# Row sums of the adjacency: added up over tiles by VectorE and GpSimd, with TensorE summing over partitions alone

## The chip, the core and the metric

The kernel runs on one core of a Trainium2 chip. A core has five engines that work side by side, each with its own queue of instructions in a fixed order: TensorE (PE in the profile, with its weight loads as PEld), VectorE (DVE), ScalarE (ACT), GpSimd (POOL) and SyncE (SP), which here only starts transfers. They wait for one another through semaphores. Data lies in SBUF and in the matmul banks of PSUM, both of 128 partitions[...]. The metric is the device time of one execution in microseconds (us), from the first to the last instruction.

## What is computed

Four graph layers run one after the other over x, 16 batches (B) of 1024 nodes (N) with 256 features (D), with one adjacency matrix adj of 1024 x 1024 per batch, all in fp32. Each layer normalises x, applies relu, computes an update and adds it to x. The change touches the first two layers, cut here to what matters:

```
h  = relu(layernorm(x))                              # layer 0
hw = h @ W_w.T + W_b
u  = adj * exp(e[:, None] + f[None, :] + a_b)        # f = hw @ a2
x  = x + (u / sum(u, axis=2)) @ hw

h  = relu(layernorm(x))                              # layer 1
d  = (sum(adj, axis=-1) + 1e-5) ** -0.5
x  = x + (d[:, None] * adj * d[None, :]) @ (h @ weight) + bias
```

In layer 0 the factor exp(e) cancels between u and its row sum, so with g = exp(f) the kernel needs, per batch, the weighted row sum sum_m adj[n, m] g[m] (the denominator, "den") and the plain row sum sum_m adj[n, m] (the degree, "deg"). Layer 1 takes its scale from the degree, layer 2 its inverse. Layers 2 (a gated recurrence over nodes) and 3 (two dense matmuls) are untouched.

## The kernel before, in words

`layers_0_1` goes over the batches in a software pipeline. Iteration i does layer 0 of batch i, then layer 1 of batch i-1, and, between the parts of layer 1, `reshape` of batch i (what layer 1 will need) and `prepare` of batch i+1 (what layer 0 will need). `turn` transposes the output of layer 1 of batch i-2 for layer 2. A scheduler that comes with the tile framework fixes the order of the instructions on each engine when the kernel is built; it may move an instruction past others that it doesn't depend on. At run time each engine keeps its order, whatever waits.

A batch's adjacency lies transposed in SBUF as the tile `at`: eight tiles of 128 source nodes m (the partitions) by 1024 target nodes n. `load` fetches x and `at` on SyncE's queue, in that order: one transfer for x, four for pairs of `at` tiles. `at` has three buffers, x four. A buffer is loaded anew when the last reader of its old content is done.

`prepare` (L169) has three steps. The first takes layernorm statistics on VectorE (L133, L134), and the inverse root on GpSimd (`rs`, L68). The second makes the relu q and, with L178, the dot product f on VectorE, and adds a bias to x on GpSimd (L180); ScalarE makes g = exp(f) (L182), which it writes into column 0 of a tile `gs` of 32 columns per adjacency tile. Column 1 of `gs` holds ones, the others zeros. The third multiplies rs by g (`rg`, L185) on VectorE and scales q with that on ScalarE (L187).

`layer_0` (L190) first makes the row sums on TensorE (`pd`, L196): for each half of the target nodes, eight matmuls with 32 stationary columns of `gs`, one per adjacency tile, four of them side by side in TensorE's column groups (32 columns each). The result lies in PSUM as rows: row 32k has a part of den and row 32k+1 a part of deg. ScalarE copies it to `ds` (L198). Then come the neighbour sums in four parts (`sums`, L147 to L158): a part is eight matmuls of 512 columns into one of two PSUM banks `pa`, which ScalarE (L155) or VectorE (L157) copies to `ag`; a part can begin when the bank of the part before the last has been copied. Eight small matmuls with `sel` (L206) then turn `ds` into columns, one target node per partition, and add the four row groups. VectorE takes the reciprocal of den (L208) and a copy of deg (L210), and the projection by w0 (L214) is added to x with that scale (L215). From deg come `dis_v` (L64), `dis` by GpSimd (L68) and, for layer 2, `safe` (L220 to L225).

`layer_1` has four more such parts, its own projection (L251, L252), the stores x_d and he_d by GpSimd (L254, L258) and the statistics in between. So in the order of VectorE, `prepare` of the next batch lies between the parts of layer 1, and so do the copies of the `pa` banks.

A matmul in fp32 shows as two instructions in the profile, so the 16 matmuls of the row sums show as 32.

Of the kernel before, what the change touches and what calls it, by code (L numbers as in the profile page):

```python
# [9 lines left out]
F32 = mybir.dt.float32  # L10
AF = mybir.ActivationFunctionType
ALU = mybir.AluOpType
AX = mybir.AxisListType
# [3 lines left out]
P = 128  # L17
B, N, D, H = 16, 1024, 256, 1024
NT = N // P
# [19 lines left out]
def gnn_stack(ctx: ExitStack, tc: tile.TileContext, a: dict, out: bass.AP):  # L39
    nc = tc.nc  # L40
# [3 lines left out]
    ident = const.tile([P, P], F32, name="ident")  # L44
    make_identity(nc, ident)
    ones = const.tile([P, P], F32, name="ones")
# [10 lines left out]
    def rows(ap):  # L57
        return ap.rearrange("(t p) d -> p t d", p=P)

    def inv_sqrt(pool, src, eps, shape, name, mul=1.0):  # L60

        t = pool.tile(shape, F32, name=name + "_v")
        if mul == 1.0:
            nc.vector.tensor_scalar(t, src, eps, None, op0=ALU.add)  # L64
        else:
            nc.vector.tensor_scalar(t, src, mul, eps, op0=ALU.mult, op1=ALU.add)
        r = pool.tile(shape, F32, name=name)
        nc.gpsimd.tensor_tensor(r, t, mhalf.to_broadcast(shape), ALU.pow)  # L68
        return r
# [23 lines left out]
    def layers_0_1():  # L93
        with ExitStack() as st:
            wp = st.enter_context(tc.tile_pool(name="w01", bufs=1))
            big = st.enter_context(tc.tile_pool(name="big01", bufs=1))
            small = st.enter_context(tc.tile_pool(name="small01", bufs=2))
            psum = st.enter_context(tc.tile_pool(name="psum01", bufs=2, space=PSUM))
# [19 lines left out]
            v = wp.tile([P, D + 1], F32, name="v")  # L118
            nc.vector.tensor_copy(v, pv)

            gs = [wp.tile([P, NT, 32], F32, name=f"gs{i}") for i in range(2)]
            for g in gs:
                nc.vector.memset(g, 0.0)
                nc.vector.memset(g[:, :, 1:2], 1.0)
            sel = wp.tile([P, 2], F32, name="sel")
            nc.vector.tensor_reduce(sel, ident.rearrange("p (q r) -> p r q", r=32)[:, :2], AX.X, ALU.add)

            def stats(x):

                mv = small.tile([P, NT, 2], F32, name="mv")  # L130
                for t in range(NT):
                    s6 = small.tile([P, 6], F32, name="s6", bufs=4)
                    nc.vector.bn_stats(s6, x[:, t])  # L133
                    nc.vector.bn_aggr(mv[:, t], s6)  # L134
                rs = inv_sqrt(small, mv[:, :, 1], LN_EPS, [P, NT], "rs")
                return mv, rs
# [10 lines left out]
            def sums(at, h, ag):  # L147

                def part(n0, c):
                    pa = psum.tile([P, 512], F32, name="pa")  # L150
                    for mt in range(NT):
                        nc.tensor.matmul(pa, h[:, mt, c * P : (c + 1) * P], at[:, mt, n0 : n0 + 512],  # L152
                                         start=mt == 0, stop=mt == NT - 1)
                    if c == 0:
                        nc.scalar.copy(ag[:, c, n0 : n0 + 512], pa)  # L155
                    else:
                        nc.vector.tensor_copy(ag[:, c, n0 : n0 + 512], pa)  # L157
                return [lambda n0=n0, c=c: part(n0, c) for n0 in (0, 512) for c in range(DC)]  # L158

            at, x, q, g, h1, h2, dis = {}, {}, {}, {}, {}, {}, {}  # L160

            def load(b):
                x[b] = big.tile([P, NT, D], F32, name="x", bufs=4)
                nc.sync.dma_start(x[b], rows(a["x"][b]))
                at[b] = big.tile([P, NT, N], F32, name="at", bufs=3)
                for t in range(0, NT, 2):
                    nc.sync.dma_start(at[b][:, t : t + 2], rows(a["adjT"][b])[:, t : t + 2])

            def prepare(b):  # L169

                mv, rs = stats(x[b])
                yield
                q[b] = big.tile([P, NT, D], F32, name="q")
                f = small.tile([P, NT], F32, name="f")
                for t in range(NT):
                    nc.vector.tensor_scalar(q[b][:, t], x[b][:, t], mv[:, t, 0:1], 0.0, op0=ALU.subtract, op1=ALU.max)
                    junk = small.tile([P, D], F32, name="junk")
                    nc.vector.scalar_tensor_tensor(junk, q[b][:, t], rs[:, t : t + 1], v[:, :D],  # L178
                                                   op0=ALU.mult, op1=ALU.mult, accum_out=f[:, t : t + 1])
                    nc.gpsimd.tensor_tensor(x[b][:, t], x[b][:, t], vec["W_b"], ALU.add)  # L180
                g[b] = gs[b % 2]
                nc.scalar.activation(g[b][:, :, 0], f, AF.Exp, bias=v[:, D : D + 1])  # L182
                yield
                rg = small.tile([P, NT], F32, name="rg")
                nc.vector.tensor_mul(rg, rs, g[b][:, :, 0])  # L185
                for t in range(NT):
                    nc.scalar.activation(q[b][:, t], q[b][:, t], AF.Copy, scale=rg[:, t : t + 1])  # L187
                yield

            def layer_0(b, between):  # L190
                ds = big.tile([P, N], F32, name="ds")
                for n0 in (0, 512):
                    pd = psum.tile([P, 512], F32, name="pd")
                    for mt in range(NT):
                        k = mt % 4
                        nc.tensor.matmul(pd[32 * k : 32 * (k + 1)], g[b][:, mt], at[b][:, mt, n0 : n0 + 512],  # L196
                                         start=mt < 4, stop=mt >= 4)
                    nc.scalar.copy(ds[:, n0 : n0 + 512], pd)  # L198
                ag = big.tile([P, DC, N], F32, name="ag", bufs=2)
                for part in sums(at[b], q[b], ag):  # L200
                    part()
                    if between:
                        between.pop(0)()
                pn = psum.tile([P, NT, 2], F32, name="pmm")
                for nt in range(NT):
                    nc.tensor.matmul(pn[:, nt], ds[:, nt * P : (nt + 1) * P], sel, start=True, stop=True)  # L206
                rc = small.tile([P, NT], F32, name="rc")
                nc.vector.reciprocal(rc, pn[:, :, 0])  # L208
                deg = small.tile([P, NT], F32, name="deg")
                nc.vector.tensor_copy(deg, pn[:, :, 1])  # L210
                for nt in range(NT):
                    po = psum.tile([P, D], F32, name="pmm")
                    for c in range(DC):
                        nc.tensor.matmul(po, ag[:, c, nt * P : (nt + 1) * P], w0[:, c], start=c == 0, stop=c == DC - 1)  # L214
                    nc.vector.scalar_tensor_tensor(x[b][:, nt], po, rc[:, nt : nt + 1], x[b][:, nt],  # L215
                                                   op0=ALU.mult, op1=ALU.add)

                dis[b] = inv_sqrt(small, deg, DEG_EPS, [P, NT], "dis")
                zero = small.tile([P, NT], F32, name="zero")
                nc.vector.tensor_scalar(zero, deg, 0.0, None, op0=ALU.is_equal)  # L220
                safe = small.tile([P, NT], F32, name="safe")
                nc.vector.tensor_add(safe, deg, zero)
                nc.vector.reciprocal(safe, safe)
                nc.vector.tensor_scalar(zero, zero, -1.0, 1.0, op0=ALU.mult, op1=ALU.add)
                nc.vector.tensor_mul(safe, safe, zero)  # L225
                return safe
# [49 lines left out]

            nothing = lambda: None
            load(0)
            for _ in prepare(0):
                pass  # L280
# [506 lines left out]
    def layer_3():  # L787
        with ExitStack() as st:
# [113 lines left out]
            for b in range(B):  # L902
# [21 lines left out]
                nc.gpsimd.dma_start(rows(out[b]), x[b])  # L924

    layers_0_1()
    layer_2()
    layer_3()
# [49 lines left out]
```

## Time and profile before

Three runs took 5647.23, 5647.41 and 5648.99 us, the median 5647.41; the profiled run took 5646.3, its span 5644.6.

| what | us |
|---|---|
| PE busy (whole span) | 5215.2 (92%) |
| DVE busy | 2638.4 (47%) |
| POOL busy | 1418.8 (25%) |
| row sums `pd`, L196, 512 instructions | 62.1 |
| turn to columns, L206, 256 instructions | 29.5 |
| neighbour sums of layers 0 and 1, L152, 2048 instructions | 907.4 |
| idle time of PE before L152, for VectorE's copy L157 | 34.9 |
| one iteration in the middle of the stage | 78.94 |

A row of the groups reads: line, engine, operation, output and inputs, shapes, count, then busy time and mean ns, then the idle time of the engine just before these instructions and who ended it. Busy time of TensorE is an upper reading, since matmuls are pipelined; the distance from start to start in the timeline is the better measure of what a group costs. The window tables give the clock that TensorE was granted (1.00 is full).

### The profile page before, as it was taken

To read this page: it belongs to the slowest core of one execution; us is meant where nothing else is said; L and a number is where in the kernel's file an instruction comes from. 1 tells how busy PE (TensorE), PEld (TensorE's weight loads), DVE (VectorE), ACT (ScalarE), POOL (GpSimd) and SP (SyncE) were. 2 spreads that over 40 slices of the span, in tenths; PEclk is the share of its full clock that TensorE was granted. 3 is DMA by queue.
4 is the path that set the end of the run, shared out by engine and by line. 5 is a ranking of instruction groups with operands and counts; after the bars stand their busy time and mean duration, and the time that the engine had idled before them with its cause. 6 is when DMAs were issued, how large, how long until landed. Compare 5 with 4: busy or idle time off the path is not lost. (4 is left out here: it accounts for less than half of the span.)

```text
span 5644.6 us, 63144 instructions
## 1 busy us (share of the span) xinstructions
PE 5215.2 (92%) x22975; PEld 3637.5 (64%) x22975; DVE 2638.4 (47%) x6386; ACT 1393.6 (25%) x2970; POOL 1418.8 (25%) x1823
## 2 busy tenths in 40 slices
PE   6999999995799998999889999998869999999999
PEld 3455554553687787878778788787645655556555
DVE  3454444532254555555545455555544343343433
ACT  1221112110122222222222222222223232222322
POOL 2232222220111212212121211212124243342422
PEclk9999999997899999999999999999989999999999
DMA  3322332215623333233143333321032212122210
GB/s 127 117 106 77 119 119 112 92 51 154 194 81 122 86 96 100 72 109 87 55 119 93 115 92 99 105 79 40 10 126 90 92 65 105 53 105 82 75 52 16
DMA packets 471994, 520.25 MB, mean 92 GB/s; under 512 B 49793, under 2 KB 419457, under 8 KB 469377
## 3 DMA queue, kind: packets, MB, share of 16 engines
q1 hardware_dynamic: 445440, 430.75, 23.6%
q0 software_dynamic: 26112, 84.03, 4.1%
q8 instruction: 227, 3.72, 0.3%
q14 instruction: 215, 1.75, 0.1%
HBM read 430.70 MB, written 83.95 MB: 91 GB/s over the span
## 5 line engine op out<-in xcount | busy, mean ns | idle before, releaser
L414 PE MATMUL pf<-ab,hb 128*128 128x128 f32 x3648 | 517.7, 284 | 46.7 <-DMA hb<-he_d 34.4
L414 PEld LDWEIGHTS pf<-ab,hb 128*128 128x128 f32 x3648 | 492.2, 199 | 80.9 <-issue 41.1
L852 PE MATMUL ph<-ag,w 128*128 128x512 f32 x1024 | 480.4, 612 | 34.6 <-DVE hh L856 34.5
L152 PE MATMUL pa<-at,h 128*128 128x512 f32 x1024 | 459.0, 602 | 34.9 <-DVE ag L157 34.9
L837 PE MATMUL pa<-at,h 128*128 128x512 f32 x1024 | 455.1, 595 | 29.6 <-DMA at<-in_adjT 29.6
L152 PE MATMUL pa<-at,q 128*128 128x512 f32 x1024 | 448.4, 594 | 0.0
L890 PE MATMUL po<-w,hh 128*128 128x256 f32 x2048 | 447.7, 379 | 0.0
L890 PEld LDWEIGHTS po<-w,hh 128*128 128x128 f32 x2048 | 387.8, 190 | 59.3 <-issue 7.9
L152 PEld LDWEIGHTS pa<-at,h 128*128 128x128 f32 x1024 | 194.8, 193 | 272.3 <-issue 224.3
L852 PEld LDWEIGHTS ph<-ag,w 128*128 128x128 f32 x1024 | 179.2, 190 | 295.6 <-DVE hh L856 151.5
L837 PEld LDWEIGHTS pa<-at,h 128*128 128x128 f32 x1024 | 194.0, 191 | 261.9 <-issue 259.9
L629 DVE TENSOR_TENSOR r<-r,x 128x256 f32<-128x256 f32 x450 | 187.3, 428 | 336.6 <-ACT r L628 336.6
L152 PEld LDWEIGHTS pa<-at,q 128*128 128x128 f32 x1024 | 191.1, 190 | 237.3 <-issue 237.3
L858 POOL TENSOR_TENSOR ss<-ss,sq 128x512 f32<-128x512 f32 x224 | 305.1, 1362 | 116.0 <-ACT sq L855 111.5
L586 PE MATMUL pr<-dx,wh 128*128 128x256 f32 x1288 | 312.7, 386 | 7.5 <-DVE dx L603 7.4
L744 POOL TENSOR_TENSOR ho<-ho,dh 128x512 f32<-128x512 f32 x64 | 81.2, 1269 | 940.0 <-DVE dh L647 785.0
L628 ACT ACTIVATE r<-pr 128x256 f32<-128x256 f32 x450 | 148.2, 381 | 644.7 <-PE pr L586 600.9
L586 PE MATMUL pz<-wh,dx 128*128 128x256 f32 x1288 | 304.7, 379 | 0.0
L586 PE MATMUL pc<-wh,drx 128*128 128x256 f32 x1288 | 304.5, 379 | 0.0
L157 DVE COPY ag<-pa 128x512 f32<-128x512 f32 x64 | 44.2, 690 | 488.0 <-PE pa L152 488.0
L586 PEld LDWEIGHTS pc<-wh,drx 128*128 128x128 f32 x1288 | 244.6, 190 | 33.6 <-DVE drx L631 0.3
L586 PEld LDWEIGHTS pr<-dx,wh 128*128 128x128 f32 x1288 | 235.8, 193 | 46.8 <-issue 13.6
(170 smaller groups left out, 8480.6 us busy)
## 6 DMA issues: line engine op xcount, KB each, us to landing
at<-in_adjT SPq DMA_DIRECT2D x128, 1024.0 KB
ab<-in_adj SPq DMA_DIRECT2D x128, 512.0 KB
x<-in_x SPq DMA_DIRECT2D x16, 1024.0 KB
x_d<-x POOLq DMA_DIRECT2D x16, 1024.0 KB, 7.9
he_d<-h POOLq DMA_DIRECT2D x16, 1024.0 KB, 7.9
heT_d<-hT POOLq DMA_DIRECT2D x16, 1024.0 KB, 4.2
he<-heT_d SPq DMA_DIRECT2D x16, 1024.0 KB
hb<-he_d SPq DMA_DIRECT2D x16, 1024.0 KB
```

The costliest lines, as they stand in the source:

```text
L152: nc.tensor.matmul(pa, h[:, mt, c * P : (c + 1) * P], at[:, mt, n0 : n0 + 512], start=mt == 0, stop=mt == NT - 1)
L157: nc.vector.tensor_copy(ag[:, c, n0 : n0 + 512], pa)
L414: nc.tensor.matmul(pb[:, c], hb[:, j, c * P : (c + 1) * P], ab[:, j], start=j == jts[0], stop=j == jts[-1])
L586: nc.tensor.matmul(to, lhsT, rhs, start=False, stop=True, skip_group_check=True)
L628: nc.scalar.activation(r[:, e], pr[:, e], AF.Sigmoid)
L629: nc.vector.tensor_mul(r[:, e], r[:, e], x[:, e])
L744: nc.gpsimd.tensor_tensor(ho, ho, dh, ALU.add)
L837: nc.tensor.matmul(pa, h[b][:, mt, c * P : (c + 1) * P], at[b][:, mt, n0 : n0 + NH], start=mt == 0, stop=mt == NT - 1)
L852: nc.tensor.matmul(ph, w1[:, c, k * P : (k + 1) * P], ag[:, c, n0 : n0 + NH], start=c == 0, stop=c == DC - 1)
L858: nc.gpsimd.tensor_tensor(ss, ss, sq, ALU.add)
L890: nc.tensor.matmul(po, hh[:, c, k * P : (k + 1) * P], w2[:, c], start=c == 0, stop=c == HC - 1)
```

## The change

The sum over m is split. Over the eight tiles it is done away from TensorE: VectorE builds den by scaling the first tile with g and adding the other seven with one multiply-add each, and GpSimd builds deg by seven additions. Both lie in a tile `both` of two rows of 1024 values per partition, in one buffer. TensorE is left with the sum over the 128 partitions: four matmuls with 32 columns of ones, each with its own 512 values and its own column group, after the second part of the neighbour sums instead of ahead of the first. The turn to columns then takes four matmuls with four columns of the identity. To make room in SBUF, x has three buffers instead of four, and the `gs` tiles and the two-buffer `ds` go away. The change is meant to free TensorE of most of the row sums.

```diff
--- before.py
+++ after.py
@@ -118,12 +118,9 @@
             v = wp.tile([P, D + 1], F32, name="v")
             nc.vector.tensor_copy(v, pv)
 
-            gs = [wp.tile([P, NT, 32], F32, name=f"gs{i}") for i in range(2)]
-            for g in gs:
-                nc.vector.memset(g, 0.0)
-                nc.vector.memset(g[:, :, 1:2], 1.0)
-            sel = wp.tile([P, 2], F32, name="sel")
-            nc.vector.tensor_reduce(sel, ident.rearrange("p (q r) -> p r q", r=32)[:, :2], AX.X, ALU.add)
+
+            sel = wp.tile([P, 4], F32, name="sel")
+            nc.vector.tensor_copy(sel, ident[:, ::32])
 
             def stats(x):
 
@@ -157,10 +154,10 @@
                         nc.vector.tensor_copy(ag[:, c, n0 : n0 + 512], pa)
                 return [lambda n0=n0, c=c: part(n0, c) for n0 in (0, 512) for c in range(DC)]
 
-            at, x, q, g, h1, h2, dis = {}, {}, {}, {}, {}, {}, {}
+            at, x, q, both, h1, h2, dis = {}, {}, {}, {}, {}, {}, {}
 
             def load(b):
-                x[b] = big.tile([P, NT, D], F32, name="x", bufs=4)
+                x[b] = big.tile([P, NT, D], F32, name="x", bufs=3)
                 nc.sync.dma_start(x[b], rows(a["x"][b]))
                 at[b] = big.tile([P, NT, N], F32, name="at", bufs=3)
                 for t in range(0, NT, 2):
@@ -178,36 +175,44 @@
                     nc.vector.scalar_tensor_tensor(junk, q[b][:, t], rs[:, t : t + 1], v[:, :D],
                                                    op0=ALU.mult, op1=ALU.mult, accum_out=f[:, t : t + 1])
                     nc.gpsimd.tensor_tensor(x[b][:, t], x[b][:, t], vec["W_b"], ALU.add)
-                g[b] = gs[b % 2]
-                nc.scalar.activation(g[b][:, :, 0], f, AF.Exp, bias=v[:, D : D + 1])
+                g = small.tile([P, NT], F32, name="g")
+                nc.scalar.activation(g, f, AF.Exp, bias=v[:, D : D + 1])
                 yield
                 rg = small.tile([P, NT], F32, name="rg")
-                nc.vector.tensor_mul(rg, rs, g[b][:, :, 0])
+                nc.vector.tensor_mul(rg, rs, g)
                 for t in range(NT):
                     nc.scalar.activation(q[b][:, t], q[b][:, t], AF.Copy, scale=rg[:, t : t + 1])
+                both[b] = big.tile([P, 2, N], F32, name="both")
+                den, deg = both[b][:, 0], both[b][:, 1]
+                nc.gpsimd.tensor_tensor(deg, at[b][:, 0], at[b][:, 1], ALU.add)
+                nc.vector.tensor_scalar(den, at[b][:, 0], g[:, 0:1], None, op0=ALU.mult)
+                for t in range(1, NT):
+                    nc.vector.scalar_tensor_tensor(den, at[b][:, t], g[:, t : t + 1], den, op0=ALU.mult, op1=ALU.add)
+                    if t > 1:
+                        nc.gpsimd.tensor_tensor(deg, deg, at[b][:, t], ALU.add)
                 yield
 
             def layer_0(b, between):
-                ds = big.tile([P, N], F32, name="ds")
-                for n0 in (0, 512):
-                    pd = psum.tile([P, 512], F32, name="pd")
-                    for mt in range(NT):
-                        k = mt % 4
-                        nc.tensor.matmul(pd[32 * k : 32 * (k + 1)], g[b][:, mt], at[b][:, mt, n0 : n0 + 512],
-                                         start=mt < 4, stop=mt >= 4)
-                    nc.scalar.copy(ds[:, n0 : n0 + 512], pd)
                 ag = big.tile([P, DC, N], F32, name="ag", bufs=2)
-                for part in sums(at[b], q[b], ag):
+                for i, part in enumerate(sums(at[b], q[b], ag)):
                     part()
                     if between:
                         between.pop(0)()
-                pn = psum.tile([P, NT, 2], F32, name="pmm")
-                for nt in range(NT):
-                    nc.tensor.matmul(pn[:, nt], ds[:, nt * P : (nt + 1) * P], sel, start=True, stop=True)
+                    if i == 1:
+                        pd = psum.tile([P, 512], F32, name="pd", bufs=1)
+                        for k in range(4):
+                            nc.tensor.matmul(pd[32 * k : 32 * (k + 1)], ones[:, :32],
+                                             both[b][:, k // 2, k % 2 * 512 : (k % 2 + 1) * 512], start=True, stop=True)
+                        ds = small.tile([P, 512], F32, name="ds", bufs=1)
+                        nc.scalar.copy(ds, pd)
+                pn = psum.tile([P, NT // 2, 4], F32, name="pmm")
+                for t in range(NT // 2):
+                    nc.tensor.matmul(pn[:, t], ds[:, t * P : (t + 1) * P], sel, start=True, stop=True)
+
                 rc = small.tile([P, NT], F32, name="rc")
-                nc.vector.reciprocal(rc, pn[:, :, 0])
+                nc.vector.reciprocal(rc.rearrange("p (h t) -> p t h", h=2), pn[:, :, :2])
                 deg = small.tile([P, NT], F32, name="deg")
-                nc.vector.tensor_copy(deg, pn[:, :, 1])
+                nc.vector.tensor_copy(deg.rearrange("p (h t) -> p t h", h=2), pn[:, :, 2:])
                 for nt in range(NT):
                     po = psum.tile([P, D], F32, name="pmm")
                     for c in range(DC):
```

## The prediction

> **What bounds the kernel now.** Layers 0 and 1 fill the first 1318 us; the diff touches nothing later, so I carry the rest over unchanged. I read first the busy table of one steady iteration of this stage (iteration 7, from the end of the layer-1 sums, T0 = 562.60 us, to the next such end, 641.54). Columns: window, length, then PE, PEld, DVE, ACT, POOL busy with counts, PE clock, DMA share, GB/s.
>
> ```profile
> 562.60:641.54 78.94, 76.47 (x259) 40.02 (x258) 37.00 (x110) 15.95 (x33) 21.67 (x24) 1.00 0.29 107
> ```
>
> TensorE is busy 76.47 of 78.94 us. VectorE (37.0), GpSimd (21.7) and DMA (29%) are far from full: work taken from TensorE shortens the iteration, unless what replaces it sits in front of something TensorE waits for. So I read TensorE's timeline (start, length, group):
>
> ```profile
> 569.52 3.64 PE L196 MATMUL pd<-at,gs 128*32 128x512 f32 x32
> 573.09 14.00 PE L152 MATMUL pa<-at,q 128*128 128x512 f32 x32
> ...
> 602.41 1.84 PE L206 MATMUL pmm<-sel,ds 128*128 128x2 f32 x16
> 604.12 1.11 PE L214 MATMUL pmm<-w,ag 128*128 128x256 f32 x4
> ...
> 618.08 13.90 PE L152 MATMUL pa<-at,h 128*128 128x512 f32 x32
> 634.45 7.13 PE L152 MATMUL pa<-at,h 128*128 128x512 f32 x16 [2.47 <-DVE ag L157]
> ```
>
> The row sums are the first line (3.57 us start to start) and their turn to columns is the third (1.71 us). The last line is the iteration's only gap: 2.47 us, for VectorE's copy of a PSUM bank (L157). The timelines of VectorE and GpSimd show why that copy is late, and what they do to each other:
>
> ```profile
> 570.82 0.51 DVE L64 TENSOR_SCALAR rs_v<-mv 128x8 f32<-128x8 f32 x1
> ...
> 629.14 0.47 DVE L178 SCALAR_TENSOR_TENSOR junk<-q,rs,v 128x256 f32<-128x256 f32 x1
> ...
> 630.95 0.93 DVE L178 SCALAR_TENSOR_TENSOR junk<-q,rs,v 128x256 f32<-128x256 f32 x1
> ...
> 633.62 0.17 DVE L185 TENSOR_TENSOR rg<-rs,gs 128x8 f32<-128x8 f32 x1 [0.37 <-ACT gs L182]
> 633.71 0.69 DVE L157 COPY ag<-pa 128x512 f32<-128x512 f32 x1
> ```
>
> ```profile
> 570.41 0.95 POOL L254 DMA_DIRECT2D x_d<-x  x1 [18.09 <-DVE mv L134]
> ...
> 629.97 1.63 POOL L180 TENSOR_TENSOR x<-x,W_b_sb 128x256 f32<-128x256 f32 x2 [1.05 <-DVE q L176]
> ```
>
> The copy stands in VectorE's queue behind all of `prepare`, a chain that began with the reciprocal at 604.29 and runs almost without rest to 633.71: in this half VectorE sets the pace. And VectorE slows beside GpSimd: L178 takes 0.47 us alone, 0.93 beside a GpSimd add; the tiny L64 takes 0.51 us, ending as GpSimd's instruction does (elsewhere L64 is 0.15).
>
> Last, the clock after such a gap (same columns):
>
> ```profile
> 236.38:239.80 3.42, 3.42 (x6) 1.39 (x7) 0.00 (x0) 3.14 (x8) 0.00 (x0) 0.66 0.00 0
> ...
> 634.45:637.85 3.40, 3.40 (x8) 1.63 (x9) 0.00 (x0) 3.15 (x8) 0.00 (x0) 1.00 0.00 0
> ```
>
> After 5 of the 14 gaps (155.97, 236.38, 553.81, 871.57, 1110.08 us) the clock halves for a while and the 16 matmuls take 8.60 to 8.83 us instead of 7.13; after the other 9 it doesn't.
>
> [...]
>
> **The change part by part**, per steady iteration:
>
> *Removed from TensorE.* pd goes from 32 instructions to 8 (4 matmuls of two passes, still four column groups): 8 x 3.57/32 = 0.9, say 1.0 us with its start, so -2.6. The turn goes from 16 to 8 instructions: -0.85. Together -3.4 us.
>
> *Added to VectorE, ahead of the copy.* As built, VectorE's order after L185 is: the first scaling (L188 of the changed file), two multiply-adds (L190), then the bank copy TensorE waits for, then five more L190. Each L190 waits for the one before it (in place), so they don't overlap. [...] 0.74 + 1.27 + 1.2 = +3.2 us on the gap. [...] GpSimd is then idle (its last add ends at 632.96), so 3.2. Behind the copy, the other five (6.4 us) are hidden under the last seven-us part of the sums.
>
> *A longer gap.* 2.47 + 3.2 = 5.7 us[...]; before it was 5 x 1.7/14 = 0.6. +0.85; bounds 0 and 1.7.
>
> *Added to GpSimd.* Seven adds of 1024 columns. From L494 (256 columns 732 ns, 128 columns 460): 2.1 ns a column, so 2.35 us[...]; I take 2.4 with the wait on its own result, 17 us in all. GpSimd's order as built: he_d store of i-2, the seven adds for batch i+1, heT_d store, `dis` of batch i. `both` has one buffer, so the adds wait for pd of batch i: they run an iteration ahead of their use, and TensorE never waits for them. But when do they end? pd ends at T0+23. Their tile comes later than before: with three x buffers, x[i+1] may load only when h2 of batch i-2 is done (T0+15), and adjT queues behind x in the same queue. Data then starts near T0+16.7, x and he_d (2 MB) and the first adjT pair (1 MB) at the 400 GB/s of the busiest slices take 8 us: T0+24.7. So the adds run from T0+24.7 to T0+41.7. TensorE's turn now ends 3.4 us sooner, at T0+38.1, and VectorE reaches `dis_v`, `zero` and `safe` (tiny single-source and two-input SBUF operations, L64 and after) at T0+39.6. They'd sit behind the last add, as L64 did behind the store: +2.1 us. Queued behind them: the second x update (L215), for which the third PSUM bank of the projection waits, and the whole chain to the copy. So the delay goes through to the end of the iteration. Bounds: 0 (adds end by T0+39.6) and 4.
>
> *At no cost:* `sel`, the memsets (once), the strided reciprocal (8 elements), one pd bank instead of two (read once per iteration), the ds copy (ACT is idle), x with three buffers (x lands by T0+23, first read near T0+47).
>
> Sum: -3.4 + 3.2 + 0.85 + 2.1 = +2.75 us, for iterations 2 to 14: +35.8. Iterations 0 and 1: -6.8 for TensorE, +1.4 because the sums start after the first scaled q where pd started with g, +3[...], +3 of delay at `dis`, +3.2 of gap: +3.8. Iteration 15 has no `prepare` and no adds: -3.4. Total +36: 5683 us.
>
> **The rivals.** (1) [...]the adds end in time, or the tiny operations slip between them. 13 x 0.65 + 0.8 - 3.4 = +6: 5653. For it: during `dis` on GpSimd (605.91 to 607.58) the tiny L222 ran in 0.15. Against: `dis` is 8 elements; the adds stream 1024. (2) *Faster*: the gap grows by 2.5 only and the clock stays, 13 x -0.9 - 3 - 3.4 = -18: 5629. For it: the 9 gaps with full clock. Against: VectorE's order is fixed, and the gap more than doubles. (3) *Adds much later*: adjT lands 2 us later, or the adds are slowed by VectorE, delay 4 to 5: 13 x 5.2 + 3.8 = +71: 5718. For it: L178 once took 2.89 us beside three short GpSimd operations. Against: little of VectorE runs then.
>
> **How the numbers follow.** Forecast 0.52, rival 1 0.23, rival 2 0.12, rival 3 0.13. Point 5683. The range leaves out the outer halves of rivals 2 and 3: 5636 to 5714. Within 0.2% is 5636 to 5659: most of rival 1, the edge of rival 2, 0.18. Faster 0.14, slower 0.68.
>
> **What would show it.** TensorE: pd 8 instructions in about 1 us, the turn 0.9. The gap before the last L149 part, released by VectorE's copy, near 5.7 us, with clock near 0.5 for some of the next 3.4 us. L64 of `dis_v` or L225 stretched to 1 to 2.5 us, ending as an add ends, and TensorE waiting 2 us inside the projection. Wrong if the gap stays near 2.5, if the adds end before the turn, or if TensorE waits at pd for GpSimd.

## The result and the profile after

The changed kernel took 5668.93 us (median of six runs, 5649.84 to 5681.16), the kernel before 5647.32 beside it: a ratio of 1.0039, 95% interval 1.0021 to 1.0057. It is slower by some 22 us, so the forecast had the direction and its range holds the time; 5683 was 14 us too high. How much of the working was right is another matter, and the profile tells it.

First the window table of one iteration after the change (columns as in the prediction: window, length, busy times with counts of PE, PEld, DVE, ACT, POOL, clock, DMA share, GB/s), with the first 3.4 us after one of the gaps:

```profile
568.03:571.43 3.40, 3.40 (x4) 1.50 (x5) 3.33 (x3) 0.00 (x0) 0.00 (x0) 0.50 0.00 0
...
496.40:577.40 81.00, 75.30 (x227) 39.36 (x226) 46.57 (x118) 15.35 (x32) 38.05 (x31) 0.96 0.29 104
```

The iteration is 81.0 us long, where one took 78.9 before (79.6 in the mean, with the clock losses), with 32 fewer TensorE instructions. VectorE has 9.6 us more work and GpSimd 16.4, yet neither is anywhere near full. TensorE's timeline of the same iteration (T0, the end of the layer-1 sums, is 496.4) shows where the time went:

```profile
487.91 8.55 PE L149 MATMUL pa<-at,h 128*128 128x512 f32 x16 [5.71 <-DVE ag L154]
496.30 7.11 PE L256 MATMUL pmm<-w,ag 128*128 128x256 f32 x32
...
517.95 1.07 PE L204 MATMUL pd<-both,ones 128*32 128x512 f32 x8
...
533.66 0.95 PE L210 MATMUL pmm<-sel,ds 128*128 128x4 f32 x8
534.47 1.11 PE L219 MATMUL pmm<-w,ag 128*128 128x256 f32 x4
...
568.03 9.44 PE L149 MATMUL pa<-at,h 128*128 128x512 f32 x16 [5.70 <-DVE ag L154]
```

From T0 to the end of the turn it is 38.1 us where it was 41.5: TensorE's saving is there in full, 3.5 us. From the end of the turn to the start of the gap it is 27.9 us in both kernels: no delay arises there. The gap is 5.70 us instead of 2.46, and the 16 matmuls behind it take 9.44 us instead of 7.13. All 14 gaps cost clock now; the durations behind them run 8.55, 9.44, 9.90, 10.13, and again 8.55. VectorE's timeline holds the cause of the gap and, for this iteration, the absence of the predicted delay:

```profile
535.62 0.48 DVE L220 SCALAR_TENSOR_TENSOR x<-pmm,rc,x 128x256 f32<-128x256 f32 x1 [0.72 <-PE pmm L219]
536.02 0.16 DVE L64 TENSOR_SCALAR dis_v<-deg 128x8 f32<-128x8 f32 x1
...
536.50 0.15 DVE L227 TENSOR_TENSOR safe<-deg,zero 128x8 f32<-128x8 f32 x1
...
563.90 0.17 DVE L182 TENSOR_TENSOR rg<-rs,g 128x8 f32<-128x8 f32 x1 [0.37 <-ACT g L179]
563.99 0.75 DVE L188 TENSOR_SCALAR both<-at,g 128x1024 f32<-128x1024 f32 x1
564.77 2.60 DVE L190 SCALAR_TENSOR_TENSOR both<-at,g,both 128x1024 f32<-128x1024 f32 x2
567.29 0.68 DVE L154 COPY ag<-pa 128x512 f32<-128x512 f32 x1
```

The three operations between `rg` and the copy make up the added 3.2 us. `dis_v` and `safe` are not stretched here. GpSimd's timeline says why, and the issues on SyncE's queue say where its timing comes from:

```profile
519.14 2.33 POOL L187 TENSOR_TENSOR both<-at 128x1024 f32<-128x1024 f32 x1 [6.60 <-PE pd L204]
521.55 14.47 POOL L192 TENSOR_TENSOR both<-both,at 128x1024 f32<-128x1024 f32 x6
535.96 0.59 POOL L279 DMA_DIRECT2D heT_d<-hT  x1
```

```profile
496.53 2.27 SPq L164 DMA_DIRECT2D at<-in_adjT  x4
513.23 0.37 SPq L161 DMA_DIRECT2D x<-in_x  x1
```

The additions begin when `pd` has read `both` (T0 + 22.7), not when their data come, and end at T0 + 39.6, just as `dis_v` begins; so it is in every iteration from the third on. In the first two the last addition still runs when `dis_v` begins, and `dis_v` is stretched to 0.90 and 0.95 us and ends with it. The first of them, VectorE and GpSimd:

```profile
69.42 0.90 DVE L64 TENSOR_SCALAR dis_v<-deg 128x8 f32<-128x8 f32 x1
```

```profile
67.94 2.35 POOL L192 TENSOR_TENSOR both<-both,at 128x1024 f32<-128x1024 f32 x1
```

The adjacency is asked for at T0, before x. That the order of SyncE's queue has changed against the source, where a batch's x comes before its `at`, shows where the third and fourth batch are loaded, after the change and before it:

```profile
24.53 149.69 SPq L164 DMA_DIRECT2D at<-in_adjT  x8
188.76 0.37 SPq L161 DMA_DIRECT2D x<-in_x  x1
```

```profile
35.39 1.31 SPq L164 DMA_DIRECT2D x<-in_x  x1
164.60 2.06 SPq L167 DMA_DIRECT2D at<-in_adjT  x4
```

In the changed kernel the fourth batch's `at` follows the third's, and its x comes behind them; before the change its x stood ahead of its `at`.

### The profile page after: what moved, and what is told of

It is laid out like the page before. It is cut to its first block, busy times and chain, and to the rows that moved or that the text cites. A ratio compares the mean times of both kernels' runs of the same rounds, so it can differ in the third digit from the quotient of the medians.

```text
span 5679.2 us, 62411 instructions
## 1 busy us (share of the span) xinstructions
PE 5191.5 (91%) x22463; PEld 3630.0 (64%) x22463; DVE 2805.0 (49%) x6510; ACT 1383.9 (24%) x2954; POOL 1683.5 (30%) x1935
## 5 line engine op out<-in xcount | busy, mean ns | idle before, releaser
L419 PE MATMUL pf<-ab,hb 128*128 128x128 f32 x3648 | 520.9, 285 | 52.3 <-DMA hb<-he_d 38.1
L149 PE MATMUL pa<-at,h 128*128 128x512 f32 x1024 | 483.2, 628 | 79.8 <-DVE ag L154 79.8
L842 PE MATMUL pa<-at,h 128*128 128x512 f32 x1024 | 455.2, 595 | 29.4 <-DMA at<-in_adjT 29.4
L651 DVE TENSOR_TENSOR w<-w,hc 128x256 f32<-128x256 f32 x450 | 189.5, 421 | 153.6 <-ACT hc L650 153.6
```

What stands on the lines that cost most here:

```text
L419: nc.tensor.matmul(pb[:, c], hb[:, j, c * P : (c + 1) * P], ab[:, j], start=j == jts[0], stop=j == jts[-1])
L651: nc.vector.tensor_mul(w[:, g], w[:, g], hc[:, g])
L842: nc.tensor.matmul(pa, h[b][:, mt, c * P : (c + 1) * P], at[b][:, mt, n0 : n0 + NH], start=mt == 0, stop=mt == NT - 1)
```

## The experiments

The theory after the trace: what costs is the place of three VectorE operations ahead of a bank copy, through the gap and the clock loss behind it; GpSimd's additions cost at the start alone. In the table, the base period is the usual distance of two gaps less the clock loss in it (the time over 7.13 us behind a gap), the period the mean of 13 such distances, and the mean loss the difference of the two; so it also holds what else slowed single iterations, up to 0.13 us (TensorE + 1.2). The end of the stage is the start of the last layer-1 projections. These four come from one profiled execution of each kernel; they tell kernels apart more finely than the whole time, which moves by up to 36 us from run to run.

| kernel | base period | mean loss | period | end of stage | ratio to before (95%) |
|---|---|---|---|---|---|
| before | 78.94 | 0.66 | 79.60 | 1310.1 | 1 |
| changed | 78.70 | 2.32 | 81.02 | 1334.8 | 1.0039 (1.0021 to 1.0057) |
| weighted sum late | 75.40 | 0.39 | 75.79 | 1262.3 | 0.990 (0.9885 to 0.9916) |
| gap only, 5.9 us | 82.36 | 2.84 | 85.20 | 1389.6 | 1.0114 (1.0099 to 1.013) |
| one addition of seven | 78.77 | 2.47 | 81.24 | 1330.5 | 1.0017 (1.0009 to 1.0024) |
| one addition more | 80.21 | 1.92 | 82.13 | 1355.9 | 1.007 (1.0056 to 1.0083) |
| TensorE + 0.4 | 79.14 | 2.63 | 81.77 | 1346.3 | 1.004 (1.0026 to 1.0053) |
| TensorE + 1.2 | 80.03 | 2.00 | 82.03 | 1349.5 | 1.0054 (1.0041 to 1.0068) |
| gap only, 3.2 us | 79.73 | 1.19 | 80.92 | 1328.6 | 1.0029 (1.0021 to 1.0038) |
| gap only, 4.6 us | 81.04 | 2.07 | 83.11 | 1359.8 | 1.0072 (1.0045 to 1.0098) |
| start mended | 75.39 | 0.26 | 75.65 | 1260.4 | 0.9894 (0.9879 to 0.9909) |
| copy on ScalarE | 72.74 | 0 | 72.74 | 1220.7 | 0.9824 (0.981 to 0.9837) |

### The place in VectorE's queue

`normed` records the instruction that makes `shift`, `prepare` gets a fourth step, and the sums are queued behind layer 1's `shift` (`issue_after` places them there):

```diff
+                yield
+                with tc.issue_after(shifts[-1]) if b >= 2 else nullcontext():
+                    nc.gpsimd.tensor_tensor(deg, at[b][:, 0], at[b][:, 1], ALU.add)
+                    nc.vector.tensor_scalar(den, at[b][:, 0], g[:, 0:1], None, op0=ALU.mult)
...
-                    between += [lambda: next(rows_of)] * 3
+                    between += [lambda: next(rows_of)] * 4
```

> The changed kernel, with VectorE's eight operations for the weighted row sum queued behind the `shift` of layer 1 instead of ahead of the bank copy (iterations with batch 2 and later); nothing is left out. Theory A (the place in VectorE's queue costs the time): the gap before the last part of the layer-1 sums goes from 5.70 back to 2.5 us, most of these parts run at the full clock again (mean loss 0.6 instead of 2.3 us), and the period falls from 81.0 to about 76.1 us (79.6 of before, less 3.5): the total near 5600 us, a ratio to before of about 0.992. Rival B (the added work on VectorE and GpSimd costs the time wherever it stands[...]): period 79.5 to 81, ratio 1.000 to 1.004.

The timelines of TensorE and VectorE:

```profile
464.40 7.13 PE L151 MATMUL pa<-at,h 128*128 128x512 f32 x16 [2.40 <-DVE ag L156]
```

```profile
538.99 0.17 DVE L184 TENSOR_TENSOR rg<-rs,g 128x8 f32<-128x8 f32 x1 [0.37 <-ACT g L181]
539.07 0.68 DVE L156 COPY ag<-pa 128x512 f32<-128x512 f32 x1
```

The copy follows `rg` directly, the gap is 2.40 us, and 4 of 14 gaps cost clock. VectorE does the same work (46.68 us per iteration, 46.57 in the changed kernel), GpSimd too (38.07 and 38.05), and its additions keep their place, 22.8 us behind the start of the layer-1 projections. The period is 5.2 us shorter. Theory A holds, rival B falls: the same edit with its VectorE work further back in the queue is faster than before by 1.0%.

### The gap alone

In the kernel before, with x in three buffers to make room:

```diff
                 nc.vector.tensor_mul(rg, rs, g[b][:, :, 0])
...
+                extra = big.tile([P, N], F32, name="extra")
+                nc.vector.tensor_scalar(extra, at[b][:, 0], rg[:, 0:1], None, op0=ALU.mult)
+                for t in (1, 2):
+                    nc.vector.scalar_tensor_tensor(extra, at[b][:, t], rg[:, t : t + 1], extra, op0=ALU.mult, op1=ALU.add)
```

> The kernel before (row sums on TensorE, as before) with x in three buffers and three VectorE operations of 1024 columns, whose result nobody reads, put between `rg` and the bank copy: the gap alone, without anything else of the change. Theory A: the gap goes from 2.46 to 5.7 us in every iteration that prepares a batch, every last part of the layer-1 sums loses clock as in the changed kernel (8.55 to 10.13 us for its 16 matmuls), +3.25 + 1.7 = +5.0 us for each of 14 gaps: +70 us, ratio 1.0123. The prediction's size of the clock term (0.85): +57 us, 1.010. Rival B (the clock follows from the added GpSimd and VectorE load of the changed kernel, not from the gap): +45 us, 1.008.

Two gaps late in the stage:

```profile
1181.96 10.08 PE L152 MATMUL pa<-at,h 128*128 128x512 f32 x16 [5.89 <-DVE ag L157]
1267.28 10.09 PE L152 MATMUL pa<-at,h 128*128 128x512 f32 x16 [5.90 <-DVE ag L157]
```

The gap is 5.9 us, the loss 2.8 us in the mean, without any of the changed kernel's GpSimd work. The end of the stage comes 79.5 us later in the profile, which is that of the slowest of the four runs, and the whole time grows by 1.14%, 64 us (70 expected, 57 by the prediction's clock term, 45 by rival B). The clock loss follows from the gap.

### GpSimd's additions, fewer and more

One kernel leaves out six of the seven additions; the other does the first one twice:

```diff
-                    if t > 1:
-                        nc.gpsimd.tensor_tensor(deg, deg, at[b][:, t], ALU.add)
```

```diff
-                nc.gpsimd.tensor_tensor(deg, at[b][:, 0], at[b][:, 1], ALU.add)
+                for _ in range(2):
+                    nc.gpsimd.tensor_tensor(deg, at[b][:, 0], at[b][:, 1], ALU.add)
```

> The changed kernel without six of the seven GpSimd additions for each batch: the plain row sum then covers two of eight tiles, everything else is unchanged. Theory A (GpSimd's additions cost only at the start[...]): the first layer-0 sums for batch 0 are followed by pd some 5 to 9 us sooner, the period stays at 81.0 us; total -5 to -10 us against the changed kernel, ratio to before 1.002 to 1.003. Rival B (the additions slow VectorE or TensorE in every iteration): the period falls by 0.5 us or more, ratio below 1.001.

> The changed kernel with the first GpSimd addition of each batch done twice, the same result: the additions then end 2.4 us later, near 42 us after the end of the layer-1 sums, past the point (39.6 us) where VectorE comes to the tiny operations behind the turn. Theory P ([...]): `dis_v` or its neighbours stretch to 1 to 2.5 us, the x updates behind them and the whole chain to the bank copy slip by about 2 us, the period goes from 81.0 to 83, ratio to before about 1.009. Rival Q (no such collision at all, or it is absorbed): period 81.0, ratio 1.003 to 1.005.

With fewer, the base period is the same (78.77, 78.70), and the whole gain lies at the start: the first gap ends at 155.55 us instead of 163.34 (before: 155.97), 1.5 us of it because the first transfers landed sooner in that run (the first matmul ran at 9.69 us instead of 11.15). Of these 7.8 us a larger clock loss takes back 2.9 (periods of 81.24 and 81.02). The start in the changed kernel, TensorE and VectorE:

```profile
36.30 15.94 PE L149 MATMUL pa<-at,q 128*128 128x512 f32 x32 [23.09 <-ACT q L184]
```

```profile
26.14 2.55 DVE L175 SCALAR_TENSOR_TENSOR junk<-q,rs,v 128x256 f32<-128x256 f32 x1
...
28.61 3.15 DVE L173 TENSOR_SCALAR q<-x,mv 128x256 f32<-128x256 f32 x2
...
33.86 1.84 DVE L182 TENSOR_TENSOR rg<-rs,g 128x8 f32<-128x8 f32 x1 [0.37 <-ACT g L179]
35.63 0.74 DVE L188 TENSOR_SCALAR both<-at,g 128x1024 f32<-128x1024 f32 x1
36.40 15.12 DVE L190 SCALAR_TENSOR_TENSOR both<-at,g,both 128x1024 f32<-128x1024 f32 x7
```

The same lines with one addition:

```profile
29.00 16.09 PE L149 MATMUL pa<-at,q 128*128 128x512 f32 x32 [17.26 <-ACT q L184]
```

```profile
28.24 0.17 DVE L182 TENSOR_TENSOR rg<-rs,g 128x8 f32<-128x8 f32 x1 [0.37 <-ACT g L179]
28.32 0.75 DVE L188 TENSOR_SCALAR both<-at,g 128x1024 f32<-128x1024 f32 x1
29.11 9.21 DVE L190 SCALAR_TENSOR_TENSOR both<-at,g,both 128x1024 f32<-128x1024 f32 x7
```

`rg`, of eight columns, begins beside an addition and takes 1.84 us instead of 0.17, until the addition ends. Of the seven multiply-adds three meet additions and take 3.25 to 3.26 us, the other four 1.29. L173, a scaling with one tile as input, is held as well: the second of the two shown takes 2.42 us instead of 0.34 and ends at 31.76, just behind an addition (31.61). L188, a scaling too, takes the same 0.75: it began 0.13 us ahead of the next addition (35.63 and 35.76), so it doesn't show how a scaling fares behind one. Theory A holds.

With one addition more, VectorE, GpSimd and TensorE show the collision that the prediction had put into the changed kernel:

```profile
713.25 0.16 DVE L64 TENSOR_SCALAR dis_v<-deg 128x8 f32<-128x8 f32 x1
713.32 0.17 DVE L226 TENSOR_SCALAR zero<-deg 128x8 f32<-128x8 f32 x1
713.39 0.42 DVE L130 BATCH_NORM_STATS2 s<-x 128x6 f32<-128x256 f32 x1
713.73 1.99 DVE L228 TENSOR_TENSOR safe<-deg,zero 128x8 f32<-128x8 f32 x1
```

```profile
710.91 2.35 POOL L193 TENSOR_TENSOR both<-both,at 128x1024 f32<-128x1024 f32 x1
713.34 2.36 POOL L193 TENSOR_TENSOR both<-both,at 128x1024 f32<-128x1024 f32 x1
```

```profile
713.50 1.89 PE L220 MATMUL pmm<-w,ag 128*128 128x256 f32 x8
716.64 4.58 PE L220 MATMUL pmm<-w,ag 128*128 128x256 f32 x20 [1.25 <-DVE x L221]
```

`safe`, which adds two SBUF tiles of eight columns, stands 1.99 us until the last addition ends at 715.7; TensorE waits for the x update behind it, and the way from the turn to the gap grows from 27.9 to 29.4 us. So the mechanism of theory P is there, at 1.5 us of base period; the changed kernel escapes it with nothing to spare, since its last addition ends at 536.02 us, where `dis_v` begins. But the period grew by 1.1 only, not 2, since the clock loss shrank from 2.32 to 1.92.

`dis_v` and `zero` ran at full speed here because they began between two additions: at 713.25 and 713.32, where one addition ended at 713.26 and the next began at 713.34. In the first two iterations of this kernel, as of the changed one, `dis_v` began while an addition ran and was held to its end (0.89 and 0.96 us). So both kinds that the prediction named were held, tiny scalings and operations with two SBUF inputs. Not held beside an addition were the statistics (L130, 0.42 us above, 0.39 to 0.43 in the changed kernel) and the x update, whose other input lies in PSUM (0.48 us at 535.62 in the changed kernel, as at other times). Why the first two kinds are held and these are not, no run here shows.

### The clock term: a grid

With one addition more, the late periods are 81.91 to 81.93 us; with the gap alone they go to 85.33. The window table of the changed kernel has the granted clock, in quarters of a us, where it falls and where it returns:

```profile
487.25:487.50 0.25, 0.00 (x0) 0.00 (x0) 0.25 (x2) 0.25 (x2) 0.00 (x0) 0.76 0.00 0
487.50:487.75 0.25, 0.00 (x0) 0.00 (x0) 0.25 (x1) 0.25 (x1) 0.00 (x0) 0.50 0.00 0
...
490.50:490.75 0.25, 0.25 (x2) 0.12 (x1) 0.25 (x1) 0.00 (x0) 0.00 (x0) 0.50 0.00 0
490.75:491.00 0.25, 0.25 (x2) 0.16 (x1) 0.25 (x1) 0.00 (x0) 0.00 (x0) 0.91 0.00 0
```

It falls at 487.38 and returns at 490.79, close to the gap's end plus twice the loss (487.91 + 2 x 1.42 = 490.75): at a clock of 0.50 each two us lose one. This return and the next four, read in the same way, are at 490.79, 572.71, 654.64, 736.56 and 815.06 us, that is 81.92, 81.93, 81.92 and 78.50 apart. All 14 returns, from 166.53 to 1221.25 us, lie within 0.01 us of a grid with a step of 3.413 us, worked out from them: 1054.72 us in 309 steps. The five returns of the kernel before (158.96, 240.88, 558.32, 875.76 and 1114.69 us) are 24, 93, 93 and 70 such steps apart. The stretches at 0.50 last one step or two: 3.41 us in 3 cases and 6.82 or 6.83 in 11 after the change, 3.41 or 3.42 in all 5 before. The distances above are 24, 24, 24 and 23 steps, and 85.33 is 25. So in these executions the clock falls and returns on a fixed grid. A gap that ends later against the grid has a shorter slow stretch behind it and loses half of the difference less: the deviation halves each time (with the gap alone the losses are 2.12, 2.54, 2.75, 2.86, 2.91 and 2.93 us on the way to 2.96), and the loss settles where base plus loss is a whole number of steps (82.36 + 2.96 = 85.32). To try this, matmuls of the turn were repeated, two or six per batch:

```diff
-                for t in range(NT // 2):
+                for t in [0, 1] + list(range(NT // 2)):
                     nc.tensor.matmul(pn[:, t], ds[:, t * P : (t + 1) * P], sel, start=True, stop=True)
```

```diff
-                for t in range(NT // 2):
+                for t in [0, 1, 2, 3, 0, 1] + list(range(NT // 2)):
```

> The changed kernel with the first two matmuls of the turn done twice (four more instructions on TensorE, 0.41 us per batch, the same result): a probe of the clock term. Theory W (the clock is decided on a fixed grid of 3.413 us, at which its returns stand in the changed kernel's profile, so that the loss settles where the period is a whole number of grid steps, if a loss of 1.40 to 3.08 us allows it): base 78.70 + 0.41 = 79.11 us, loss 2.81, period 81.92 = 24 steps in the late iterations; +0.9 us against the changed kernel's 81.02, +12 us over 13. Rival L (a mean loss of 2.3 us whatever the period, so that work adds as it is): period 81.43, +5 us.

> The changed kernel with six matmuls of the turn done twice (twelve more instructions on TensorE, 1.22 us per batch, the same result). Theory W (grid of 3.413 us): base 79.92 us, loss 2.00, period 81.92 as with 0.41 us more, so that 0.8 us of TensorE's work per batch cost nothing. Rival L (a mean loss): period 82.24, +16 us over 13 against the changed kernel, 11 us more than with 0.41.

The last gaps with 0.4 us more, and with 1.2:

```profile
1145.25 9.91 PE L149 MATMUL pa<-at,h 128*128 128x512 f32 x16 [5.69 <-DVE ag L154]
1227.18 9.91 PE L149 MATMUL pa<-at,h 128*128 128x512 f32 x16 [5.70 <-DVE ag L154]
```

```profile
1148.43 9.02 PE L149 MATMUL pa<-at,h 128*128 128x512 f32 x16 [5.69 <-DVE ag L154]
1230.35 9.02 PE L149 MATMUL pa<-at,h 128*128 128x512 f32 x16 [5.69 <-DVE ag L154]
```

Both stand at 81.92 us, with losses of 2.78 and 1.89: the 0.9 us between them are paid back by the clock. Theory W holds, L falls (81.43 and 82.24). The whole times don't show it: 5670.0 and 5678.6 lie 8.5 us apart, nearer to L's 11 than to nothing, but the runs of each kernel spread over 8 and 11 us. The stage ends, of one execution each, lie 3.2 us apart (1346.3 and 1349.5; 1334.8 in the changed kernel). The changed kernel itself would need a loss of 81.92 - 78.70 = 3.22 us, more than any seen there (3.0), so it can't settle and goes round in four iterations.

Two shorter gaps, made as in the kernel with the gap alone but with one extra operation (no loop) or two, ask from which length on a gap costs:

```diff
-                for t in (1, 2):
+                for t in (1,):
```

> The kernel before with x in three buffers and one VectorE operation of 1024 columns, whose result nobody reads, ahead of the bank copy: the gap grows by about 0.75 to 3.2 us, less than one grid step of 3.413 us. Theory W [...]: [...]7 to 9 of 14 gaps are followed by a loss of 1.7 us (5 of 14 at 2.46 us); period 79.71 + 1.0 = 80.7, ratio near 1.003. Rival L (any gap over 2.5 us costs clock each time): 14 of 14, period 81.4, ratio 1.004 to 1.005.

> As before, with two such operations ahead of the bank copy: a gap of 4.5 to 4.7 us. Theory W[...]: nearly every gap costs, no loss under 1.4, mean 1.6 to 1.7 us; period 81.0 + 1.7 = 82.7, ratio 1.007 to 1.009. Rival S[...]: losses from 0.6 to 1.7, mean 1.3 us, period 82.3.

At 3.24 us the loss is 1.70 or nothing, as at 2.46: it comes after 10 of 14 gaps (7 to 9 expected, 14 by rival L). At 4.57 us all 14 cost, none under 1.4, as W has it and rival S has not; but the mean is 2.1, above both (1.6 to 1.7, and 1.3), with losses near 1.4, 1.7 and 2.85 in turn. The counts and losses expected here were the author's estimates.

How much idle time goes ahead of a drop is shown by the 28 gaps of the kernel before and the changed one, laid on the grid of their clock's returns. A step at full clock that held 2.14 us or more of a gap was followed by a step at 0.50, and one that held 1.90 us or less was not. A step at 0.50 was followed by another when it held 0.72 us or more of the gap, and by the full clock when it held 0.54 us or less. Whether gaps of other lengths keep to these figures wasn't shown.

### Towards a faster kernel

The start was mended by queuing batch 0's sums behind the last bias addition, and its `pd` behind the fourth part:

```diff
+                with tc.issue_after(shifts[-1]) if b >= 2 else tc.issue_after(bias_add) if b == 0 else nullcontext():
...
-                    if i == 1:
+                    if i == (1 if b else 3):
```

> The kernel with the late weighted sum, and for batch 0 GpSimd's additions queued behind its last bias addition, VectorE's eight operations with them, and pd of batch 0 behind the fourth part of its sums; nothing is left out. Theory A ([...]): the first layer-0 sums start near 29.5 us as with six additions left out (29.00) instead of 34.8 to 37.0, the end of the stage comes 5 to 7 us sooner than with the late weighted sum alone (1262.3), ratio to before 0.989. Rival B (the start is set by the adjT transfers or by ScalarE): no change, first sums near 35.

The first sums start at 29.48 us as expected, but the stage ends only 1.9 us sooner, and that through two clock losses instead of four: the first gap even ends 1.6 us later (161.09 and 159.45). GpSimd and VectorE after that:

```profile
66.96 12.04 POOL L196 TENSOR_TENSOR both<-both,at 128x1024 f32<-128x1024 f32 x5
...
79.68 1.70 POOL L68 TENSOR_TENSOR rs<-rs_v,mhalf 128x8 f32<-128x8 f32 x1
```

```profile
81.41 0.17 DVE L246 TENSOR_TENSOR rd<-rs,dis 128x8 f32<-128x8 f32 x1 [6.76 <-POOL rs L68]
```

The additions for batch 1 wait for batch 0's later `pd`, and now stand in GpSimd's queue ahead of the `rs` that `reshape` needs: the 5.3 us gained are given back, with a wait of 6.8 us where the kernel with the late sum has 1.3. Theory A, that the additions hold up VectorE's work ahead of the first sums, is right on the cause and wrong on the gain.

Last, the copy of the second part's bank, for which TensorE waits, goes to ScalarE, ahead of the exponential in its queue (`early` holds that copy; layer 1 alone sets `spare`):

```diff
-                    if c == 0:
-                        nc.scalar.copy(ag[:, c, n0 : n0 + 512], pa)
+                    if c == 0 or (spare and n0 == 0):
+                        copied = nc.scalar.copy(ag[:, c, n0 : n0 + 512], pa).ins
+                        if spare and c == 1:
+                            early[:] = [copied]
...
+                with tc.issue_after(early[0]) if early else nullcontext():
+                    nc.scalar.activation(g, f, AF.Exp, bias=v[:, D : D + 1])
```

> As the kernel with the start mended, and the bank copy that TensorE waits for is done by ScalarE, ahead of the exponential in its queue; nothing is left out. Theory A (that copy's place behind VectorE's `prepare` work is the only reason for the remaining gap of 2.4 us): no gap, no clock loss in the last part, period 75.4 - 2.4 = 73.0 us, total near 5645 - 13 x 6.6 = about 5560 us, ratio 0.984. Rival B (VectorE's chain is itself too long and another wait takes the gap's place, at the start of the next layer-0 sums): period 74 to 75.4, ratio 0.987 to 0.989.

```profile
509.27 20.77 PE L151 MATMUL pa<-at,h 128*128 128x512 f32 x48
529.88 7.11 PE L263 MATMUL pmm<-w,ag 128*128 128x256 f32 x32
```

The parts run through without a gap, no clock is lost, and the period is 72.74 us (457.14 to 529.88). The whole kernel takes 5547.4 us, 1.8% less than before: theory A. Part of that is a gap which the kernel before had too; the change's own saving on TensorE, 3.5 us per iteration, shows in the kernel with the late sum (base period 75.40 instead of 78.94).

## Why the prediction was right, and where it was not

Per steady iteration, the terms as put and as measured:

| term | predicted | measured | shown by |
|---|---|---|---|
| TensorE, `pd` and turn | -3.4 | -3.47 | timeline after |
| three VectorE operations ahead of the copy | +3.2 | +3.24 | timeline after; late sum; gap only |
| clock behind the longer gap | +0.85 | +1.66 | gap only; grid |
| tiny operations held by the additions | +2.1 | 0 (from the third iteration on) | timeline after; one addition more |
| sum | +2.75 | +1.43 | period: +1.42 |

Times 13 that is 18.5 us of the 24.7 at the end of the stage. The rest is +7.4 up to the first gap's end (predicted +3.8 for iterations 0 and 1; 0.8 of the 7.4 is that the first matmul ran at 11.15 us and not at 10.32) and -1.2 behind the last one (predicted -3.4). The other layers, which the change doesn't touch, were 10 us longer in the profiled execution (spans of 5679.2 and 5644.6 us), which the medians don't show.

The main bet held: work is hidden or not by its place in the queue, not by how busy its engine is. VectorE at half load took back nearly all that TensorE had gained, the clock the rest and more, and the late sum shows that it was the place. The prices of the three VectorE operations, 0.74, 1.27 and 1.2 us, were the author's estimates; the trace after has 0.75, and 2.60 for the last two together.

The step that failed is "adjT queues behind x in the same queue ... So the adds run from T0+24.7 to T0+41.7." `load` lists x first, but the scheduler had put the adjacency ahead of it; x itself was asked for at T0 + 16.8, as worked out, but the data of the additions were there, the additions started at `pd`'s end and ended at T0 + 39.6. The 27 us of the forecast that rest on it (13 x 2.1) fell away. The order of SyncE's queue in the built kernel would have told it; the prediction read VectorE's and GpSimd's order as built, but this one from the source. The mechanism was right, `dis_v` included: in iterations 0 and 1 it was held for 0.7 and 0.8 us (+3 predicted for both), and with one addition more, 2.4 us later, the delay costs 1.5 us in every iteration.

The clock term was half of what it should be. The predicted mean loss, 0.85 us above that of before, was the author's estimate, which no trace of before showed; the loss is 2.3 us, and it isn't an average over positions of the gap, since the period adjusts itself to the grid (81.92 us with 0.4 and with 1.2 us more on TensorE). That the total came near was luck: this error (+10.5 us over 13 iterations), the start (+3.6) and the last iteration (+2.2) made up for more than half of the failed step (-27). Rival 1 (the additions end in time, 5653) is what happened in the steady iterations, and its 16 us too few are in the main the same clock term and the same start; the measured time lies about midway between it and the forecast. The sum of rival 3 leaves out the -3.4 of the last iteration: it gives 5715, not 5718.

The start was mis-sized because the additions for batch 0 were priced as if `pd` alone waited for them. They also held VectorE's `prepare`, so that TensorE was idle for 23.1 us ahead of its first sums and not 17.3 as with one addition: 5.8 us.

## What to carry to other kernels

Before moving work to a half-idle engine, look at what stands behind it in that engine's queue: 3.2 us ahead of one copy, with the clock lost behind it, outweighed the 3.5 us saved, and the same work behind the copy left the saving whole (base period 75.40, 3.5 us under that of before). Read the order of every queue from the built kernel, the one that issues transfers too. Two chains that just miss each other, as the additions and `dis_v` do here, are a risk to be named: 2.4 us more work on an engine with half of its time free cost 1.5 us. A gap on TensorE cost its length and, in these traces at times from 2.4 us and always from 4.6 us on, clock on top; where one remains, small changes elsewhere can vanish in it (0.9 us of TensorE's work did), and removing the gap was worth more than its length (2.9 us per iteration for one of 2.4).

## What the runs showed of the hardware

- At a gap the granted clock was 0.50 for 3.41 or 3.42 us, or for 6.82 or 6.83, and its returns lay on a grid with a step of 3.413 us (1054.72 us in 309 steps in the changed kernel).
- With a gap of 5.7 or 5.9 us in every iteration, the periods of four kernels settled at 81.92 or 85.33 us, 24 or 25 of these steps; 0.9 us more TensorE work per iteration then left the period the same.
- In 28 gaps of the kernel before and the changed one, a step at full clock with 2.14 us or more of the gap in it was followed by a step at 0.50, one with 1.90 us or less was not.
- Gaps of 2.4 us cost clock in 2 or 4 of 14 cases, of about 2.46 in 5, of about 3.24 in 10, of about 4.57 and of 5.7 to 6.2 us in all; in gaps of up to 3.53 us the loss was 1.5 to 1.7 us or none, in those of 4.56 us and more 1.4 to 3.1.
- VectorE operations that began while an addition of GpSimd ran were held to its end: those with two SBUF inputs, `rg` and `safe` (1.84 and 1.99 us for eight columns instead of 0.17 and 0.15), and scalings of one SBUF tile (0.90 and 0.95 instead of 0.16 for eight columns, 2.42 instead of 0.34 for 256). The scaling of 1024 columns that began ahead of an addition wasn't (0.74 us); nor were the statistics (0.42 us) and the x update that reads PSUM (0.48).
